# Latent attention moved to the ends of each slot, the block table cut in three, and 42 products of constants in a two-layer decoder on one core

## The chip, the core and the metric

The kernel runs on one core of a Trainium2 chip. The metric is the time of one execution in device microseconds (us). The kernel before has a median of 1145.13 us over four runs (1139.52 to 1148.7).

The engines by the profile's names: PE (TensorE matrix products; PEld is its weight load), DVE (VectorE), ACT (ScalarE), POOL (GpSimd) and SP (SyncE, which here only issues DMAs). Each engine works through its own queue in the order in which the program issued the instructions.

## What is computed

A decoder of two layers over 32 sequences of 128 tokens with 128 features. Three residual steps per layer, each with a layer norm in front:

```python
x = x + L0_attn(layernorm(x))        # 16 heads, rotary
x = x + L0_xattn(layernorm(x), ctx)  # 16 heads over 128 context tokens
x = x + L0_ffn(layernorm(x))         # gated experts, 2 of 8, and 2 shared
x = x + L1_attn(layernorm(x))        # 16 heads, rotary, causal
x = x + L1_xattn(ctx, latents=layernorm(x), mask)
x = x + L1_ffn(layernorm(x))         # relu experts, 2 of 8
```

The change touches the last two steps. `L1_xattn`, the "latent attention", has two heads of 64: queries are the normalised tokens, keys are those same tokens and 128 masked context tokens, 256 keys in all.

```python
q = ln @ Wq.T
kv = concatenate([xn @ Wkv.T, ln @ Wlkv.T])
attn = softmax(mask(rmsnorm(q) @ rmsnorm(k)))
out = attn @ v @ Wo.T + bo
```

`L1_ffn` sends each token to two of eight experts of 512 hidden features: `gate * (relu(x @ w1 + b1) @ w2 + b2)`.

## The kernel before

The 32 sequences form 8 groups (`G`) of 4 (`NG`), whose activations stay in SBUF. The three 16-head attentions run as one pipeline, written out by hand: `attention` walks over slots `k`, two slots to a sequence, 192 slots in all. A slot has the phases `open`, `pre`, then the slot's own score products and exponentials (L602 to L645), `inner`, the products with the values of an earlier pair (L661), `turn`, `turned`, `mid`, `post`. All other work is registered with `at(slot, phase, function)`, and is issued in that order; within one phase in the order of registration. The last products with values are in slot 197; after it a slot holds only what `at` put there.

The latent attention (`latent_attention`) starts for group g at slot d = 147 + 8g. After norm and projection (L1121) each of its four sequences takes four steps, at t = d + 8 + 2i for sequence i: `turn` (L1186, transposes queries and keys, which ACT copies out, L1188 and L1189) in slot t, `score` (products L1195 and L1200, maximum on DVE L1206, exponential on ACT L1207) in t + 1, `turn_e` (transposes L1214, copy on DVE L1216) in t + 2, `weigh` (products with the values L1226, division on DVE L1231 and L1232) in t + 3. `fetch` (L1181) has loaded the context's values in slot t - 2 into one of three buffers, and so waits for the `weigh` of three sequences before. `leave` (L1161) and `project` (L1168) end the group in d + 18 and d + 19. So a sequence begins every second slot from 155 to 217, with `turn` and `turn_e` in odd slots, `score` and `weigh` in even ones. All four steps are in `mid`.

The products of these steps, of norms, projections and routers share three PSUM banks (`ps_m`), taken in turn: an allocation waits until the readers of the third one before it are done; `score` takes two. The attention's own scores have two banks (`ps_s`), their transposed second form two (`ps_t`), and the sums one (`ps_a`).

After the latent attention `router` picks two experts for each token of groups (0,1), (2,3), (4,5), (6), (7), and writes the tokens by 16 or 8 indirect DMAs of POOL (`scatter`, L1729) into slots of an expert in DRAM. `expert_blocks` then works on blocks of 128 such rows, in three parts: groups 0 to 3 with 39 blocks, 4 and 5 with 23, 6 and 7 with 23. `table` (L1826 to L1852) works out on DVE, from the counts, which expert and which rows each block has. A pair of blocks takes a slot: `fetch` loads rows (L1868), `weights` copies an expert's first weights (L1877 on ACT, L1879 on DVE) out of `all_w`, `turn` transposes (L1887, copy L1889), `hidden` (L1897) and `result` (L1914) are the products, `leave` (L1928) the scatter back on POOL. `experts` gives the slots: the parts begin at `begins` = 209, 229 and 241, the table four slots earlier in `mid`; `keep` loads the eight experts' weights in slots 203 to 210 (L1966, L1967).

In `attention` (L298) `awake` issues products of an identity with itself, 128x512 in bf16, at the start of the program; nobody reads them.

Of the kernel before, what the change touches and what calls it, by code (L numbers as in the profile page):

```python
# [11 lines left out]
F32 = mybir.dt.float32  # L12
# [10 lines left out]
P = 128  # L23
# [3 lines left out]
G = B // NG  # L27
H, DH = 16, 8
E = 8
# [84 lines left out]
def decoder(ctx: ExitStack, tc: tile.TileContext, a: dict, out: bass.AP):  # L114
    nc = tc.nc
# [6 lines left out]
    ps_t = ctx.enter_context(tc.tile_pool(name="ps_t", bufs=2, space=PSUM))  # L122
# [6 lines left out]
    def bank(pool):  # L129
        return pool.tile([P, 512], F32, tag="bank", name="bank")  # L130
# [112 lines left out]
    ident_b = cpool.tile([P, P], BF16, tag="ident_b", name="ident_b")  # L243
# [3 lines left out]
    def wide(t, shape, axis):  # L247
        return t.unsqueeze(axis).to_broadcast(shape)
# [809 lines left out]
    def latent_attention(lazy, kv, row, bias, masked, plan_route):  # L1058
# [12 lines left out]
        def plan_group(at, g, d):  # L1071
# [98 lines left out]
                nc.vector.tensor_tensor(xf, ps, xf, ALU.add)  # L1170

            at(d + 18, "mid", leave)
            at(d + 19, "post", project)
            plan_route(at, g, d + 19)

        def plan_batch(at, m, g, i, t):
            b, s = g * NG + i, {}

            def fetch():
                s["kv"] = opened().tile([P, KV], F32, tag="kv", name="lkv", bufs=3)  # L1180
                nc.sync.dma_start(s["kv"][:, P:], kv[b : b + 1].rearrange("b p w -> p (b w)"))  # L1181

            def turn():
                ps = bank(ps_m)
                for n in range(2):
                    nc.tensor.transpose(ps[:, n * P : (n + 1) * P], m["qk"][:, i, n, :], ident)  # L1186
                s["qT"] = opened().tile([P, P], F32, tag="qT", name="lqT")
                nc.scalar.activation(s["qT"], ps[:, :P], AF.Identity, scale=g_qk)  # L1188
                nc.scalar.copy(s["kv"][:, :P], ps[:, P : 2 * P])  # L1189

            def score():
                sc = [bank(ps_m) for _ in range(HL)]
                rows = [slice(DL * h, DL * h + DL) for h in range(HL)]
                for h in range(HL):
                    nc.tensor.matmul(  # L1195
                        sc[h][:, P : 2 * P], ident_b[:B, b : b + 1].to_broadcast([B, P]), masked,
                        start=True, stop=False, skip_group_check=True,
                    )
                for h in range(HL):
                    nc.tensor.matmul(  # L1200
                        sc[h][:, : 2 * P], s["qT"][rows[h], :], s["kv"][rows[h], : 2 * P], start=False, stop=True, skip_group_check=True,
                    )
                mx = small.tile([P, HL], F32, tag="lmx", name="lmx")
                s["e"] = opened().tile([P, HL, 2 * P], F32, tag="e", name="le", bufs=2)
                for h in range(HL):
                    nc.vector.tensor_reduce(mx[:, h : h + 1], sc[h][:, : 2 * P], AX.X, ALU.max, negate=True)  # L1206
                    nc.scalar.activation(s["e"][:, h, :], sc[h][:, : 2 * P], AF.Exp, bias=mx[:, h : h + 1])  # L1207

            def turn_e():
                tp = bank(ps_m)  # L1210
                for h in range(HL):
                    for c in range(2):
                        n = 2 * h + c
                        nc.tensor.transpose(tp[:, n * P : (n + 1) * P], s["e"][:, h, c * P : (c + 1) * P], ident)  # L1214
                s["eT"] = opened().tile([P, 4, P], F32, tag="eT", name="leT", bufs=2)
                nc.vector.tensor_copy(s["eT"].rearrange("p n k -> p (n k)"), tp)  # L1216

            def weigh():
                if i == 0:
                    m["on"] = opened().tile([P, NG, D], F32, tag="on", name="lon", bufs=1)  # L1220
                vc = s["kv"][:, 2 * P :].rearrange("p (h w) -> p h w", h=HL)
                av = bank(ps_m)[:, : HL * (DL + 1)].rearrange("p (h w) -> p h w", h=HL)
                for h in range(HL):
                    for c in range(2):
                        v = m["v"][:, i, h, :] if c == 0 else vc[:, h, :]
                        nc.tensor.matmul(  # L1226
                            av[:, h, :], s["eT"][:, 2 * h + c, :], v,
                            start=(h == 0 and c == 0), stop=(c == 1), skip_group_check=True,
                        )
                rz = small.tile([P, HL], F32, tag="lrz", name="lrz")  # L1230
                nc.vector.reciprocal(rz, av[:, :, DL])  # L1231
                nc.vector.tensor_tensor(  # L1232
                    m["on"][:, i, :].rearrange("p (h d) -> p h d", d=DL), av[:, :, :DL], wide(rz, [P, HL, DL], 2), ALU.mult
                )

            at(t - 2, "mid", fetch)
            at(t, "mid", turn)
            at(t + 1, "mid", score)
            at(t + 2, "mid", turn_e)
            at(t + 3, "mid", weigh)  # L1240

        def beside(at, done):
            for g in range(G):
# [575 lines left out]
    def expert_blocks(f, total, lazy):  # L1819

        room, nb, top_slot = ROOM[f], NB[f], SLOTS[f] - BLOCK
        y = tc.dram_tile([2 * room, D], F32, name=f"y{f}")
        state = {}
        where = []

        def table():  # L1826

            def row(shape, tag, dtype=F32):
                return lazy["blocks"].tile([1] + shape, dtype, tag="tb_" + tag, name="tb_" + tag, bufs=2 if tag == "where" else 1)

            count, blocks, end, skip = row([E], "count"), row([E], "blocks"), row([E], "end"), row([E], "skip")
            nc.vector.tensor_tensor(count, total[:1], e_base[f][:1], ALU.subtract)
            more = row([E, room // BLOCK], "more")
            nc.vector.tensor_tensor(
                more, wide(count, [1, E, room // BLOCK], 2), wide(starts[:1, : room // BLOCK], [1, E, room // BLOCK], 1), ALU.is_gt
            )
            nc.vector.tensor_reduce(blocks, more, AX.X, ALU.add)
            upto = row([E, E], "upto")
            nc.vector.tensor_tensor(upto, wide(blocks, [1, E, E], 1), until[:1], ALU.mult)
            nc.vector.tensor_reduce(end, upto, AX.X, ALU.add)  # L1840
            nc.vector.tensor_scalar(skip, blocks, -float(BLOCK), float(room), ALU.mult, ALU.add)
            past, t = row([nb, E], "past"), row([nb, E], "past_t")
            first = row([3, nb], "first")
            nc.vector.tensor_tensor(past, wide(end, [1, nb, E], 1), wide(numbers[:1, :nb], [1, nb, E], 2), ALU.is_le)
            nc.vector.tensor_reduce(first[:, 0, :], past, AX.X, ALU.add)
            nc.vector.tensor_tensor(t, past, wide(skip, [1, nb, E], 1), ALU.mult)
            nc.vector.tensor_reduce(first[:, 1, :], t, AX.X, ALU.add)
            nc.vector.tensor_tensor(first[:, 1, :], first[:, 1, :], starts[:1, :nb], ALU.add)
            nc.vector.tensor_scalar(first[:, 2, :], first[:, 0, :], float(E - 1), 512.0, ALU.min, ALU.mult)
            nc.vector.tensor_scalar(first[:, 0, :], first[:, 0, :], float(E - 1), float(W1), ALU.min, ALU.mult)  # L1850
            where.append(row([3, nb], "where", I32))
            nc.vector.tensor_copy(where[0], first)  # L1852
# [95 lines left out]
            nc.gpsimd.tensor_tensor(one, one, two, ALU.add)  # L1948
            nc.vector.tensor_tensor(X[g], X[g], one, ALU.add)

        return table, fetch, weights, turn, hidden, result, leave, gather, finish

    def experts(halves, lazy, heads, late):

        def beside(at, done):
# [4 lines left out]
            def keep(e):  # L1960
                def fn():
                    rows = a["w_f"][e * P : (e + 1) * P]
                    if e == 0:
                        for tag, n in (("w1", W1), ("w2", 512)):
                            lazy[tag] = lazy["blocks"].tile([P, E * n], F32, tag=tag, name="all_" + tag, bufs=1)
                    nc.sync.dma_start(lazy["w1"][:, e * W1 : (e + 1) * W1], rows[:, :W1])  # L1966
                    nc.sync.dma_start(lazy["w2"][:, e * 512 : (e + 1) * 512], rows[:, W1:])  # L1967
                return fn

            at(done(2, G - 1) + 2, "open", swap)  # L1970
            for e in range(E):
                at(done(2, G - 1) + 2 + e, "open", keep(e))
            begins = [done(2, 3) + 40]
            begins.append(max(begins[0] + (NB[0] + 1) // 2, done(2, 5) + 40))
            begins.append(max(begins[1] + (NB[1] + 1) // 2, done(2, 7) + 33))

            def plan_part(f):
                table, fetch, weights, turn, hidden, result, leave, gather, finish = halves[f]
                t = begins[f]
                pairs = (NB[f] + 1) // 2  # L1980
                at(t - 4, "mid", table)
                for i in range(4):
                    at(t, "post", lambda i=i: fetch(i))
                for i in range(2):
# [95 lines left out]
    lazy, late = {}, ExitStack()  # L2080
# [123 lines left out]
```

## Time and profile before

| | us |
|---|---|
| median of four runs | 1145.13 |
| the profiled execution, its own time | 1146.88 |
| its span, first to last instruction | 1145.2 |
| last products with values (slot 197) begin | 856.4 |
| first `hidden` product (slot 211) begins | 917.3 |
| last `result` product ends | 1110.8 |

| engine | busy us | share |
|---|---|---|
| PE | 1046.9 | 91% |
| DVE | 823.7 | 72% |
| POOL | 646.1 | 56% |
| ACT | 616.1 | 54% |

The mean granted TensorE clock is 0.957. The span falls into the attention pipeline up to 857 us, a bridge of 14 slots (197 to 210) up to 917, the blocks up to 1112, and a tail with the last scatters, the gathering of the results and the stores. Rows of an engine's timeline give the start, the duration, the line, output<-input, and in square brackets how long the engine had been idle before and what ended that; "issue" is idle time without a wait.

### The profile page before, as it was taken

How to read it: one execution, taken by the hardware profiler on the slowest of the kernel's cores; microseconds unless marked ns; L12 is line 12 of the kernel's file. 1: busy time of each engine (PE TensorE's matmuls, PEld its weight loads, DVE VectorE, ACT ScalarE, POOL GpSimd, SP SyncE). 2: the span in 40 equal slices, each digit the busy share in tenths (PEclk: the TensorE clock that was granted, in tenths of full speed). 3: DMA queues.
4: the chain of work that ended last, by engine and by line, in shares of the span. 5: the costliest groups of instructions: out<-in, count | busy, mean ns of one | idle time of the engine just before them, and what ended most of it. 6: DMA issues, size and time to landing. Idle time of an engine off the chain costs nothing.

```text
span 1145.2 us, 32419 instructions
## 1 busy us (share of the span) xinstructions
PE 1046.9 (91%) x12495; PEld 817.0 (71%) x12495; DVE 823.7 (72%) x2424; ACT 616.1 (54%) x1440; POOL 646.1 (56%) x918
## 2 busy tenths in 40 slices
PE   6999999999999999999998999998997899989893
PEld 3676676777777766766676667776775588989893
DVE  4678888877787678667877768887767656766662
ACT  2355555566755565546554666674563445445551
POOL 4576666534524462444555765764884716777663
PEclk9889989999999999999999999999999679999997
DMA  7663331000120221011102000000102522223432
GB/s 205 200 192 104 104 104 63 30 29 30 38 48 5 46 48 38 10 30 39 39 3 52 2 16 16 16 12 20 39 25 81 153 53 58 65 74 98 123 98 79
DMA packets 77858, 71.24 MB, mean 62 GB/s; under 512 B 14554, under 2 KB 66829, under 8 KB 77696
## 3 DMA queue, kind: packets, MB, share of 16 engines
q1 hardware_dynamic: 72640, 60.08, 19.2%
q0 software_dynamic: 4768, 8.47, 2.2%
q8 instruction: 102, 1.67, 0.6%
q14 instruction: 60, 0.49, 0.1%
q10 hardware_dynamic: 288, 0.52, 0.1%
HBM read 33.39 MB, written 37.02 MB: 61 GB/s over the span
## 4 chain that ended last, share of the span: by engine, by line
PE 59%; DVE 17%; POOL 9%; ACT 7%; issue 4%; DMA 3%; SPq 1%; DVEq 0%; POOLq 0%; ACTq 0%
PE bank L633 13%; PE bank L661 6%; PE bank L1914 6%; PE bank L1897 5%; DVE msc L636 4%; PE bank L950 3%; POOL h L941 2%; PE bank L932 2%; DMA g<-spread 2%; ACT e L644 2%; PE bank L933 2%; PE bank L486 2%; PE bank L511 1%; PE bank L1121 1%; PE bank L298 1%
## 5 line engine op out<-in xcount | busy, mean ns | idle before, releaser
L644 ACT ACTIVATE e<-bank 128x512 f32<-128x512 f32 x384 | 207.4, 593 | 173.3 <-PE bank L633 171.7
L636 DVE TENSOR_REDUCE msc<-bank 128x4 f32<-128x512 f32 x384 | 245.0, 679 | 71.2 <-PE bank L633 68.6
L633 PE MATMUL bank<-kb,qz 32*128 32x256 f32 x1536 | 243.6, 410 | 11.7 <-DVE msc L636 9.9
L633 PE MATMUL bank<-qa,kb 32*128 32x128 f32 x3072 | 235.1, 290 | 4.0 <-ACT e L644 3.9
L633 PEld LDWEIGHTS bank<-qa,kb 32*128 32x128 f32 x3072 | 196.2, 192 | 8.1 <-ACT e L644 7.2
L633 PEld LDWEIGHTS bank<-kb,qz 32*128 32x128 f32 x1536 | 147.7, 190 | 64.1 <-DVE msc L636 32.6
L1928 POOL DMA_INDIRECT y<-bo,bx x85 | 85.2, 1002 | 63.2 <-ACT bo L1921 40.9
L647 POOL TENSOR_SCALAR_AFFINE_SELECT e<-e 128x512 f32<-128x512 f32 x128 | 79.5, 646 | 67.5 <-ACT e L644 67.2
L661 PE MATMUL bank<-e,vt 128*32 128x128 f32 x3072 | 109.6, 285 | 0.9 <-POOL e L647 0.8
L661 PEld LDWEIGHTS bank<-e,vt 128*32 128x32 f32 x3072 | 81.6, 113 | 15.9 <-POOL e L647 2.0
L1914 PE MATMUL bank<-all_w,bh 128*128 x680 | 87.8, 284 | 0.5 <-issue 0.4
L1914 PEld LDWEIGHTS bank<-all_w,bh 128*128 128x128 f32 x680 | 83.0, 199 | 2.7 <-issue 2.3
L1897 PE MATMUL bank<-bxT,w 128*128 128x128 f32 x680 | 84.9, 278 | 0.0
L1729 POOL DMA_INDIRECT slots<-rows,r_ati x64 | 63.8, 997 | 33.1 <-issue 17.4
L1897 PEld LDWEIGHTS bank<-bxT,w 128*128 128x128 f32 x680 | 81.2, 196 | 0.0
L941 POOL TENSOR_TENSOR h<-h,g 128x512 f32<-128x512 f32 x30 | 38.7, 1301 | 67.1 <-DMA g<-spread 40.4
L338 ACT ACTIVATE xn<-x,ln_nb,ln_rs 128x128 f32<-128x128 f32 x96 | 42.0, 490 | 47.4 <-POOL ln_nb L332 46.9
L1207 ACT ACTIVATE le<-bank,lmx 128x256 f32<-128x256 f32 x64 | 26.8, 470 | 60.7 <-DVE lmx L1206 60.7
L1905 DVE TENSOR_SCALAR bh<-bank,w 128x128 f32<-128x128 f32 x164 | 46.1, 343 | 17.5 <-PE bank L1897 17.0
L540 DVE SCALAR_TENSOR_TENSOR qa<-bank,head_rows,qz 128x128 f32<-128x128 f32 x192 | 57.6, 342 | 0.0
L1903 ACT ACTIVATE bh<-bank,w 128x128 f32<-128x128 f32 x176 | 50.3, 368 | 10.6 <-PE bank L1897 8.7
L1921 ACT ACTIVATE bo<-bank,bx 128x128 f32<-128x128 f32 x44 | 16.2, 367 | 65.4 <-PE bank L1914 65.4
(337 smaller groups left out, 2309.8 us busy)
## 6 DMA issues: line engine op xcount, KB each, us to landing
slots<-nowhere SPq DMA_DIRECT2D x8, 1170.0 KB, 10.9
slots<-nowhere SPq DMA_DIRECT2D x4, 2210.0 KB, 20.6
g<-spread SPq DMA_DIRECT2D x16, 512.0 KB, 5.2
bx<-slots SPq DMA_DIRECT2D x85, 65.0 KB, 1.9
kv<-kcv SPq DMA_DIRECT2D x8, 516.0 KB, 3.2
lkv<-kv SPq DMA_DIRECT2D x32, 129.0 KB, 2.1
yg<-y SPq DMA_DIRECT2D x14, 256.0 KB, 4.4
all_w<-in_w_f SPq DMA_DIRECT2D x8, 258.0 KB, 3.3
```

The costliest lines, as they stand in the source:

```text
L540: nc.vector.scalar_tensor_tensor(s["qa"][:, u, :], s["mp"], head_rows[:, 1 - u : 2 - u], m["qz"][:, u, i * P : (i + 1) * P], ALU.mult, ALU.add
L633: nc.tensor.matmul(o, l, r, start=start, stop=stop, skip_group_check=True)
L636: nc.vector.tensor_reduce(tops(MSC[bb % 4], 2 * h + j), sc[j].rearrange("p (s n k) -> p s n k", s=2, n=2), AX.X, ALU.max, negate=True)
L644: nc.scalar.activation(e.rearrange("p n q -> p (n q)"), tr[j], AF.Exp, scale=SCALE)
L647: nc.gpsimd.affine_select(out=e, in_=e, compare_op=ALU.is_ge, fill=0.0, base=0, pattern=[[0, 4], [1, P]], channel_multiplier=-1)
L661: nc.tensor.matmul(s3["av"][32 * n : 32 * n + 32, h3 * P : (h3 + 1) * P], m3["vt"][:, i3, h3, n, u, :], es[u][:, n, :], start=(h3 == 0 and ...
L941: engine.tensor_tensor(m["h"][:, c, :], m["h"][:, c, :], m["g"][:, c, :], ALU.mult)
L1729: ins = nc.gpsimd.indirect_dma_start(slots[f], bass.IndirectOffsetOnAxis(ap=m["ati"][:, c, n : n + 1], axis=0), m["rows"][c][:, n, :], Non ...
L1897: nc.tensor.matmul(ps[:, c * P : (c + 1) * P], w[:, c * P : (c + 1) * P], s["xT"][:, u * P : (u + 1) * P], start=True, stop=True)
L1903: nc.scalar.activation(h, p, AF.Relu, bias=bias)
L1914: nc.tensor.matmul(ps[:, u * P : (u + 1) * P], s["h"][:, u, c, :], lazy["w2"][:, bass.ds(at_w + c * P, P)], start=(c == 0), stop=(c == 3),)
L1928: ins = nc.gpsimd.indirect_dma_start(y, bass.IndirectOffsetOnAxis(ap=x[:, D : D + 1].bitcast(U32), axis=0), s["o"][:, u, :], None, bounds_ ...
```

## The change

Four edits: `project` goes from `post` to `mid` (`g >= 0` holds for every group); the latent steps `turn` and `score` go from `mid` to `pre` and `turn_e` and `weigh` from `mid` to `post`, in the same slots; `table` becomes three functions in `post` of three slots in a row; and three products of constants are put in each of the slots 197 to 210, 42 in all.

```diff
             at(d + 18, "mid", leave)
-            at(d + 19, "post", project)
+            at(d + 19, "mid" if g >= 0 else "post", project)
...
             at(t - 2, "mid", fetch)
-            at(t, "mid", turn)
-            at(t + 1, "mid", score)
-            at(t + 2, "mid", turn_e)
-            at(t + 3, "mid", weigh)
+            early, late = ("pre", "post") if g >= 0 else ("mid", "mid")
+            at(t, early, turn)
+            at(t + 1, early, score)
+            at(t + 2, late, turn_e)
+            at(t + 3, late, weigh)
...
-        def table():
+        def table_counts():
             count, blocks, end, skip = row([E], "count"), row([E], "blocks"), row([E], "end"), row([E], "skip")
...
             nc.vector.tensor_reduce(blocks, more, AX.X, ALU.add)
-            upto = row([E, E], "upto")
+
+        def table_ends():
+            blocks, end, skip, upto = tb["blocks"], tb["end"], tb["skip"], row([E, E], "upto")
...
             nc.vector.tensor_reduce(first[:, 0, :], past, AX.X, ALU.add)
+
+        def table_firsts():
+            past, first, skip, t = tb["past"], tb["first"], tb["skip"], row([nb, E], "past_t")
             nc.vector.tensor_tensor(t, past, wide(skip, [1, nb, E], 1), ALU.mult)
...
+            def awake():
+                nc.tensor.matmul(
+                    bank(ps_t).rearrange("p (n k) -> p n k", n=4), ident_b, wide(ident_b, [P, 4, P], 1), start=True, stop=True
+                )
+
+            for k in range(done(2, G - 1) - 4, begins[0] + 2):
+                for phase in ("open", "inner", "post"):
+                    at(k, phase, awake)
...
-                at(t - 4, "mid", table)
+                for n, table in enumerate(tables):
+                    at(t - 4 + n, "post", table)
```

Instruction by instruction, the queues of POOL and SP hold the same operations in the same order as before. PE's has 42 weight loads and 42 products more; PE, DVE and ACT issue the latent attention's operations, and DVE the table's, at other places.

More of the change, by code (lines that the diff above doesn't have):

```diff
@@ L1824, in expert_blocks, with row @@
         where = []
-        def table():
-            def row(shape, tag, dtype=F32):
-                return lazy["blocks"].tile([1] + shape, dtype, tag="tb_" + tag, name="tb_" + tag, bufs=2 if tag == "where" else 1)
+        tb = {}
+        def row(shape, tag, dtype=F32):
+            tb[tag] = lazy["blocks"].tile([1] + shape, dtype, tag="tb_" + tag, name="tb_" + tag, bufs=2 if tag == "where" else 1)
+            return tb[tag]
+        def table_counts():
             count, blocks, end, skip = row([E], "count"), row([E], "blocks"), row([E], "end"), row([E], "skip")
@@ L1841, in table @@
             nc.vector.tensor_scalar(skip, blocks, -float(BLOCK), float(room), ALU.mult, ALU.add)
-            past, t = row([nb, E], "past"), row([nb, E], "past_t")
-            first = row([3, nb], "first")
+            past, first = row([nb, E], "past"), row([3, nb], "first")
             nc.vector.tensor_tensor(past, wide(end, [1, nb, E], 1), wide(numbers[:1, :nb], [1, nb, E], 2), ALU.is_le)
             nc.vector.tensor_reduce(first[:, 0, :], past, AX.X, ALU.add)
+        def table_firsts():
+            past, first, skip, t = tb["past"], tb["first"], tb["skip"], row([nb, E], "past_t")
             nc.vector.tensor_tensor(t, past, wide(skip, [1, nb, E], 1), ALU.mult)
@@ L1949, in finish @@
             nc.vector.tensor_tensor(X[g], X[g], one, ALU.add)
-        return table, fetch, weights, turn, hidden, result, leave, gather, finish
+        return (table_counts, table_ends, table_firsts), fetch, weights, turn, hidden, result, leave, gather, finish
     def experts(halves, lazy, heads, late):
@@ L1968, in keep @@
                 return fn
+            begins = [done(2, 3) + 40]
+            begins.append(max(begins[0] + (NB[0] + 1) // 2, done(2, 5) + 40))
+            begins.append(max(begins[1] + (NB[1] + 1) // 2, done(2, 7) + 33))
+            def awake():
[5 more added lines that the diff above has]
+                    at(k, phase, awake)
             at(done(2, G - 1) + 2, "open", swap)
@@ L1972, in beside @@
                 at(done(2, G - 1) + 2 + e, "open", keep(e))
-            begins = [done(2, 3) + 40]
-            begins.append(max(begins[0] + (NB[0] + 1) // 2, done(2, 5) + 40))
-            begins.append(max(begins[1] + (NB[1] + 1) // 2, done(2, 7) + 33))
             def plan_part(f):
-                table, fetch, weights, turn, hidden, result, leave, gather, finish = halves[f]
+                tables, fetch, weights, turn, hidden, result, leave, gather, finish = halves[f]
                 t = begins[f]
                 pairs = (NB[f] + 1) // 2
-                at(t - 4, "mid", table)
+                for n, table in enumerate(tables):
+                    at(t - 4 + n, "post", table)
                 for i in range(4):
```

## The prediction

> **What bounds the kernel now.** I read the stages first (busy time in stretches), then the PE timeline for its waits, then the chain of waits, then POOL's timeline where the chain leaves PE. Columns of the first view: stretch, its length, PE, PEld, DVE, ACT, POOL busy (instructions), granted clock, DMA share, GB/s.
>
> ```profile
> 640.00:857.00 217.00, 200.66 (x2789) 155.26 (x2784) 169.88 (x482) 130.25 (x318) 147.22 (x222) 0.97 0.07 19
> 857.00:917.00 60.00, 46.95 (x269) 32.70 (x259) 41.86 (x138) 25.90 (x69) 34.66 (x44) 0.78 0.39 116
> 917.00:1112.00 195.00, 184.02 (x1550) 177.53 (x1551) 126.28 (x444) 98.60 (x278) 118.96 (x131) 0.96 0.30 82
> ...
> 884.00:900.00 16.00, 13.61 (x56) 10.04 (x57) 10.06 (x37) 6.04 (x16) 12.46 (x19) 0.50 0.77 227
> ```
>
> PE is the bound outside the bridge: 16 us idle of 217 before it, 11 of 195 after it. In the bridge PE is idle 13 of 60, and 16 us ran at half clock. So the reorder can win parts of 16 us, and the bridge is where more could lie.
>
> The waits of PE in one turn of eight slots, and the worst beside a router:
>
> ```profile
> 688.41 0.44 PE L1186 MATMUL bank<-ident,lqk 128*128 128x128 f32 x2 [0.54 <-ACT qz L456]
> 700.36 0.21 PE L1195 MATMUL bank<-masked,ident_b 32*128 32x128 bf16 x1 [0.51 <-ACT vt L491]
> 702.22 1.16 PE L1168 MATMUL bank<-w_xo,loT 128*128 128x128 f32 x8 [0.43 <-ACT le L1207]
> 712.53 1.66 PE L1121 MATMUL bank<-w_lat,lT 128*128 128x384 f32 x4 [0.71 <-DVE lon L1232]
> ...
> 784.08 0.63 PE L1111 MATMUL bank<-ident,lat 128*128 128x128 f32 x4 [2.98 <-DVE lon L1232]
> ```
>
> Each waits for a `ps_m` bank that a neighbour in the same `mid` still holds: 2.2 us per turn.
>
> The end of the bridge in the chain of waits, and POOL before it:
>
> ```profile
> 907.82 0.26 POOL r_nb L1621
> ...
> 913.17 2.85 DMA all_w<-in_w_f
> 916.04 0.43 DVE w L1879
> 916.47 0.34 DVE bxT L1889
> 916.86 0.69 PE bank L1887 x2
> 917.55 3.41 PE bank L1897 x16
> ```
>
> ```profile
> 878.01 1.68 POOL L1139 TENSOR_TENSOR nrml<-nrml,half 128x8 f32<-128x8 f32 x1 [5.22 <-DVE nrml L997]
> 879.88 1.04 POOL L1729 DMA_INDIRECT slots<-rows,r_ati  x1 [0.20 <-issue]
> ...
> 904.39 0.97 POOL L1729 DMA_INDIRECT slots<-rows,r_ati  x1 [0.30 <-issue]
> ...
> 907.82 0.26 POOL L1621 TENSOR_SCALAR r_nb<-r_nb 128x8 f32<-128x8 f32 x1
> ```
>
> From 878.0 to 908.1 POOL waits for nobody: 14 scatters at 1.28 us from start to start (17.9), two roots of 1.68, nine norm steps (4.4), a bias add (1.3), four router steps (2.6) are 29.6 of 30.1 us. Then SP issues the block fetches, 0.83 each, until 913.1, then the last weights (2.85), then copies, then L1897. From 878 on the bridge hangs on POOL and SP, whose queues the change leaves in order; PE's half clock from 884 to 900 lies beside POOL.
>
> **The change part by part.**
>
> *Latent steps to `pre` and `post`, slots 155 to 197* (some 5.2 turns of 38.8 us). Nothing is added; places change. I followed the three banks round a turn in the new order. Gone: the waits for `vt`, `le` and `lon`, because `score` takes its banks three microseconds before `values` or `project` wants one, and `weigh` a slot's end before L1121: 1.65 a turn. The `qz` wait changes place: `score` in slot 4 of the turn needs the banks of queries and keys, read by ACT for 1.49 and 0.63: 0.5. New: `score` in slot 0 needs the bank whose copy (L506, 0.58) stands on ACT behind the squares (L994, 0.63) and those behind L1122 (0.42): 1.85 after the last L1121 product against 1.0 of PE work, 0.85. New: in `pre` the latent maximum (0.75) stands on DVE ahead of the attention's own maxima (1.28), and the latent exponentials (0.84) on ACT ahead of the attention's own, for which PE's next slot waits: 0.3 by the lag of 1 to 1.5 us that I find in slot 2, nothing elsewhere. Net -2.2 + 1.65 = -0.55 a turn, -2.5 in four plain turns. By a router, the norm's transposes (L1111) now come ahead of `weigh`, so the 2.98 goes, and of the 1.8 after it I leave all: -2 net with the same new waits. Sum -4.5. Ends: -9 (no new wait) and +3 (new waits double, router gains nothing).
>
> For the first half the page's row speaks:
>
> ```profile
> L1207 ACT ACTIVATE le<-bank,lmx 128x256 f32<-128x256 f32 x64 | 26.8, 470 | 60.7 <-DVE lmx L1206 60.7
> ```
>
> ACT stands 60.7 us in front of 64 latent exponentials, as the maximum lies on DVE behind the slot's maxima and `qa`. In `pre` it lies behind the last slot's rest only.
>
> *The bridge.* POOL's run starts with the root that needs L997 (877.25). Between the router's places (to 869.98) and L997 lie 7.3 us of DVE, of which 0.69, 0.95 and 0.66 are waits for `weigh`, `score` and L1121; with `weigh` behind L997 and `score` a phase earlier I take 2.4 off. The run and what follows move by the same: -2.4. Ends: -5.2 (all of POOL's wait), and +2.6: 12 awake products of slots 197 to 200 on the path at 0.216 (twelve in 2.76 at the start).
> The other 30 products (6.5 us) I cost at nothing: PE's work in slots 201 to 207 at full-clock rows (four times 0.44 and 0.22 for `turn_e` and `turn`, three times 0.9 and 0.89 for `weigh` and `score`, 2.2 and 0.5 for the router, 0.44, 0.44, 0.9 and 1.6 for L1161, L1111, L1168, L1121) is 14 us, 18.6 with 21 constants, beside the 27.4 that POOL takes up to the last scatter. If that cover were gone they cost up to 6.5. `fetch` (L1181) now waits for a `weigh` at the slot's end, behind it on SP the weight loads and block fetches; the last went at 903.86, 2.95 ahead of the first block fetch (906.81). Two L1121 (1.9) and a product come in between, 2.1, so nothing; uncovered 2.1.
>
> *Clock.* From 884 to 900 the clock is 0.50 though PE's longest idle in the 24 us before is 1.59 us: it is the share of work, not one long gap, that let it fall. Constants raise that share. What they save on the path is the first block: 3.41 against 1.79, 1.6. In slot 214 `project` waits 1.71 for `lon` (941.63), then runs cold: 1.96 against 0.9, and the next L1914 2.59 against 1.8; `project` in `mid` comes ahead of that: up to 3.6. But PE still waits some 4 us for weights at the end of the bridge, behind the last constant. Of 5.2 I take half: -2.5; ends 0 and -5.2.
> [...]
>
> *The table.* Part 0: 3.85 us of DVE (892.96 to 896.81) beside POOL's run: 0. Part 1 (1003.89 to 1007.1): PE's next wait (1.85) is for rows that need POOL's r_nb, not the table: 0. Part 2 (1059.18 to 1063.64): PE waits 1.54 for `bxT` behind it (1065.22): -1.5, as pieces of 0.65, 1.4 and 1.55 us fit into DVE's free 1.5 us of a 3.8 us slot. Ends 0 and -3. The table is ready two slots later, still 7 us ahead of SP's use.
>
> Sum: -4.5 - 2.4 - 2.5 - 1.5 = -10.9. The profiled execution took 1146.88 (span 1145.2 and 1.7 around it): 1136.0. It lies 1.75 above the median, so 1134 against 1145.13. The terms' ends give -22 to +6; unlikely to meet, I take 1127 to 1141 as this case's own range.
>
> **The rivals.** *Slower: latent exponentials in the way.* At 723.69 ACT had waited 2.57 for the latent maximum. If in `pre` that wait stays, the attention's exponentials of 21 even slots start that much later; between such a pair's end (721.1) and the next slot's second products (722.1) is 1.0 us. 1.57 x 21 = 33 in all slots, 16 in half: with -6.4 of the other parts +10 to +27, 1155 to 1172. It decides from 0.85 us per even slot. For it: DVE is busy 78% there, its maxima ran 3 us late at 726. Against: the latent maximum passes most of that queue.
> *Much faster: PE sets the bridge.* Then clock and idle count in full: PE's busy time at full clock is some 36 of 60 (46.95 x 0.78), with constants 45, so -15 there, -8.5 elsewhere: 1121. Against it POOL's unbroken run.
> *No gain: the constants do on the path what they cost.* If DVE's steps to 873 and PE alternate, all 42 x 0.216 = 9.1 come in, in place of -2.4: 1145.7. Against it: they have no input to wait for and run while PE waits.
>
> **How the numbers follow.** Under 1% (11.5 us) cannot be told from no change here. First case 0.58, half of it beyond 1133.7; much faster 0.16; no gain 0.11; slower 0.15. Faster: 0.29 + 0.16 = 0.45; same: 0.29 + 0.11 = 0.40; slower 0.15. The range 1120 to 1150 leaves out most of the slower case and some of the fastest: 0.2.
>
> **What would show it.** PE's waits on `vt`, `le` and `lon` before L1195, L1168 and L1121 gone, new ones before L1195 on ACT `oT` and `k`, idle of L1207 well under 60; POOL's run from root to r_nb still about 30 us, beginning about 2.4 us earlier after slot 197's products; a higher clock in the bridge without a bridge shorter by more than 5 us; no PE wait on `bxT` behind the third table. It is wrong if the stretch up to slot 197 changes by over 9 us, or if POOL's run breaks.

## The result, and the profile after

| | before | after |
|---|---|---|
| median, us (runs) | 1145.92 (78) | 1149.64 (52) |
| lowest to highest | 1138.66 to 1151.49 | 1143.3 to 1159.51 |
| ratio, 95% interval | 1 | 1.0039 [1.0027, 1.0051] |
| the profiled execution, its span | 1146.88, 1145.2 | 1147.23, 1145.4 |

The changed kernel is 4.5 us slower (0.0039 x 1145.92; by the interval 3.1 to 5.8) where 11 us less were forecast. The profiled execution of after lies 2.4 us under its median, that of before 1.0 above its own, so the loss isn't seen in the two spans and has to be looked for by stages. (The last `result` product of before ends at 1125.6, not at 1110.8; in after it ends at 1125.5.) The first view is the busy time in stretches, columns as before:

```profile
640.00:857.00 217.00, 200.51 (x2798) 153.90 (x2796) 171.14 (x490) 132.12 (x321) 148.01 (x224) 0.98 0.07 19
857.00:917.00 60.00, 48.23 (x272) 31.77 (x271) 39.87 (x127) 22.99 (x60) 33.15 (x41) 0.88 0.35 104
917.00:1112.00 195.00, 183.29 (x1549) 176.92 (x1550) 125.57 (x447) 98.74 (x279) 118.58 (x131) 0.96 0.31 85
884.00:900.00 16.00, 13.02 (x69) 8.49 (x68) 7.84 (x22) 5.42 (x14) 12.78 (x19) 0.85 0.65 192
```

Between 640 and 857 PE is idle 16.5 us of 217, as before (16.3): no wait has been saved on balance. In the bridge the granted clock went from 0.78 to 0.88, and from 0.50 to 0.85 between 884 and 900. PE's timeline shows which waits took the place of the old ones:

```profile
685.45 0.21 PE L1195 MATMUL bank<-masked,ident_b 32*128 32x128 bf16 x1 [0.24 <-ACT qz L456]
685.92 0.21 PE L1195 MATMUL bank<-masked,ident_b 32*128 32x128 bf16 x1 [0.26 <-ACT k L464]
...
705.24 0.21 PE L1195 MATMUL bank<-masked,ident_b 32*128 32x128 bf16 x1 [0.62 <-DVE leT L1216]
...
710.54 0.44 PE L1226 MATMUL bank<-lv,leT 128*128 128x65 f32 x2 [0.55 <-ACT lv L1123]
...
788.27 0.66 PE L1214 MATMUL bank<-ident,le 128*128 128x128 f32 x4 [2.50 <-ACT lv L1123]
```

The first two are the forecast wait of `score` for the queries and keys, 0.50 together as forecast. The third stands where 0.85 was forecast behind the copy of `oT`, but the copy of `leT` ends it. The fourth was not forecast, and neither was the last: by a router, the 2.98 in front of L1111 is gone and 2.50 stands in front of L1214 instead. ACT's exponentials wait less, as forecast, while PE's idle total stays:

```profile
L1207 ACT ACTIVATE le<-bank,lmx 128x256 f32<-128x256 f32 x64 | 26.7, 467 | 40.3 <-DVE lmx L1206 40.3
```

In the bridge POOL's run begins 2.1 us earlier after slot 197's products with values (854.57 here, 856.37 before), and then it breaks:

```profile
874.10 1.68 POOL L1139 TENSOR_TENSOR nrml<-nrml,half 128x8 f32<-128x8 f32 x1 [5.69 <-DVE nrml L997]
...
901.30 0.97 POOL L1730 DMA_INDIRECT slots<-rows,r_ati  x1 [0.30 <-issue]
905.22 0.25 POOL L1619 TENSOR_SCALAR r_rs<-r_mv 128x8 f32<-128x8 f32 x1 [2.94 <-DVE r_mv L1614]
...
907.58 0.26 POOL L1622 TENSOR_SCALAR r_nb<-r_nb 128x8 f32<-128x8 f32 x1
```

From the start of the last scatter to that of r_nb it was 3.4 us, now 6.3. POOL waits for the router's statistics (r_mv), and these stand on DVE. Before, DVE had them ready in time:

```profile
903.25 0.28 DVE L1612 BATCH_NORM_STATS2 ln_st<-x 128x6 f32<-128x128 f32 x1
...
903.97 0.18 DVE L1613 BATCH_NORM_AGGREGATE r_mv<-ln_st 128x2 f32<-128x6 f32 x1
```

The last of them ended at 904.15, and POOL came to them at 905.44: 1.3 us to spare. After the change DVE first waits for the late `weigh`:

```profile
897.29 0.17 DVE L1231 RECIPROCAL lrz<-bank 128x2 f32<-128x2 f32 x1 [4.85 <-PE bank L1226]
```

The chain of waits shows what stands behind that. Before, its last links to SP were POOL's, from r_rs at 905.44 to r_nb; now they are DVE's.

```profile
895.76 1.50 PE bank L1226 x8
897.49 0.29 DVE lon L1232
898.14 1.59 DVE tb_skip L1847
899.74 0.40 DVE tb_past L1849
900.16 0.47 DVE tb_first L1850
901.43 0.64 DVE lqk L1122 x2
902.07 0.60 DVE leT L1216
902.67 0.39 DVE tb_past_t L1854
903.08 0.48 DVE tb_first L1855
905.12 0.32 DVE lmx L1206
...
908.07 0.30 DVE lon L1232
908.37 0.30 SPq L1863
...
...
915.32 2.63 DMA all_w<-in_w_f
...
919.48 3.42 PE bank L1905 x16
```

The second and third piece of part 0's table are links of it, 3.3 us of the tb_ rows shown; then a `lon` at 908.07, which is the `weigh` of slot 208 at the slot's end, and behind it SP's reads of the table (L1863) and block fetches. Both were costed at nothing. The products of the first block still take 3.42 (3.41 before).

### The profile page after: what moved, and what is told of

The parts are those of the page before. It is cut to its first block, busy times and chain, and to the rows that moved or that the text cites. A ratio compares the mean times of both kernels' runs of the same rounds, so it can differ in the third digit from the quotient of the medians.

```text
span 1145.4 us, 32485 instructions
## 1 busy us (share of the span) xinstructions
PE 1046.4 (91%) x12537; PEld 811.3 (71%) x12537; DVE 821.9 (72%) x2424; ACT 615.9 (54%) x1440; POOL 645.0 (56%) x918
## 3 DMA queue, kind: packets, MB, share of 16 engines
q8 instruction: 102, 1.67, 0.6%
## 4 chain that ended last, share of the span: by engine, by line
PE 52%; DVE 16%; POOL 13%; ACT 8%; issue 6%; DMA 4%; SPq 1%; POOLq 0%; DVEq 0%; ACTq 0%
PE bank L633 12%; PE bank L1922 6%; PE bank L1905 5%; PE bank L661 5%; DVE msc L636 4%; PE bank L950 3%; DMA g<-spread 3%; POOL h L941 2%; POOL slots L1730 2%; ACT e L644 2%; PE bank L932 2%; PE bank L1226 2%; POOL e L647 1%; PE bank L933 1%; PE bank L298 1%
## 5 line engine op out<-in xcount | busy, mean ns | idle before, releaser
L633 PEld LDWEIGHTS bank<-kb,qz 32*128 32x128 f32 x1536 | 145.0, 188 | 64.7 <-DVE msc L636 33.7
L647 POOL TENSOR_SCALAR_AFFINE_SELECT e<-e 128x512 f32<-128x512 f32 x128 | 79.8, 648 | 74.8 <-ACT e L644 74.7
L661 PEld LDWEIGHTS bank<-e,vt 128*32 128x32 f32 x3072 | 80.4, 112 | 14.8 <-POOL e L647 1.6
L1730 POOL DMA_INDIRECT slots<-rows,r_ati x64 | 64.0, 999 | 31.1 <-issue 16.5
```

The costliest lines, as they stand in the source:

```text
L633: nc.tensor.matmul(o, l, r, start=start, stop=stop, skip_group_check=True)
L647: nc.gpsimd.affine_select(out=e, in_=e, compare_op=ALU.is_ge, fill=0.0, base=0, pattern=[[0, 4], [1, P]], channel_multiplier=-1)
L661: nc.tensor.matmul(s3["av"][32 * n : 32 * n + 32, h3 * P : (h3 + 1) * P], m3["vt"][:, i3, h3, n, u, :], es[u][:, n, :], start=(h3 == 0 and ...
L1730: ins = nc.gpsimd.indirect_dma_start(slots[f], bass.IndirectOffsetOnAxis(ap=m["ati"][:, c, n : n + 1], axis=0), m["rows"][c][:, n, :], Non ...
```

## The experiments

All were timed against the kernel before on the same chip. The five chips differ: on two, the kernel before takes 1146 to 1147 us, on three 1179 to 1181, so ratios are compared, and stages of the blocks only between chips of one kind. The theory at the start: the late `weigh` stands on PE behind the norm's transposes (L1111), DVE waits with it, and the statistics come late to POOL. Its rival: the constants cost on the path what they take. That the pieces of parts 0 and 1 stand on DVE in front of the router's statistics and picks became the theory only after the third run.

**Parts of the change, one at a time.** Latents alone, with `project` in `mid`:

```diff
-            at(t, "mid", turn)
-            at(t + 1, "mid", score)
-            at(t + 2, "mid", turn_e)
-            at(t + 3, "mid", weigh)
+            at(t, "pre", turn)
+            at(t + 1, "pre", score)
+            at(t + 2, "post", turn_e)
+            at(t + 3, "post", weigh)
```

> The kernel before with the latent steps (and project) moved alone; table whole in mid, no constants. Theory A (the attention gains about 4 us, and the bridge gives it back because weigh, now at the end of slot 206, stands on PE behind the norm's transposes L1111, which wait for POOL; DVE waits with it, and the router's statistics and POOL's r_nb come late): slot 191 about 4 us earlier than before, r_nb no earlier than in the kernel before, first block within 2 us of before's 919.4; with the whole table still ahead of that wait, r_nb should come 1 to 3 us earlier than in the changed kernel. Time 1143 to 1149. Theory B (the 42 constants cost their 9 us on the path): clearly faster, 1138 to 1141, as the constants are not there.

Measured 0.9991 [0.9968, 1.0014]. The latents don't explain the loss, and their gain can't be told from none.

Constants alone:

```diff
+            for k in range(done(2, G - 1) - 4, begins[0] + 2):
+                for phase in ("open", "inner", "post"):
+                    at(k, phase, awake)
```

> The kernel before with the 42 products of constants alone. Theory A (POOL and SP set the bridge, PE has room): r_nb and the first block within 1 us of before, granted clock of the bridge higher, time within 2 us of before. Theory B (constants on the path): the bridge 4 to 9 us longer, time 1150 to 1155. Theory C (the clock matters): bridge 2 to 5 us shorter, time 1140 to 1143.

Measured 0.9999 [0.9979, 1.0019], with the granted clock in the bridge at 0.92.

The table alone:

```diff
-                at(t - 4, "mid", table)
+                for n, table in enumerate(tables):
+                    at(t - 4 + n, "post", table)
```

> The kernel before with the table in three pieces alone. Theory A: part 2's wait of PE for bxT (1.5 us) goes, nothing in the bridge (weigh is ahead of L1111 here, so DVE does not wait): -1 to -2 us. If the pieces themselves are what holds DVE in the bridge: r_nb 1 to 3 us later than before and time +1 to +3 us.

Measured 1.0060 [1.0037, 1.0083], 1154.51 us, 6.9 us slower, and slower than the whole change; last scatter to r_nb 6.83. Neither expectation reached that: the edit that was to gain 1.5 us is the one that loses.

The changed kernel with `weigh` of the last two groups back in `mid`:

```diff
-            at(t + 3, late, weigh)
+            at(t + 3, late if g < 6 else "mid", weigh)
```

> The changed kernel with weigh of groups 6 and 7 back in mid, all else as changed; on PE this only puts weigh ahead of L1111 in slot 206 and ahead of L1121 in slot 208 (and the like in group 7). Theory A: DVE's wait of 4.85 us for weigh goes, POOL's 2.94 us for the router's statistics goes, r_nb near 905 (changed kernel 907.6), first block 2.5 to 3.5 us earlier than in the changed kernel, time 3 to 5 us under it. Theory B (constants): no different from the changed kernel, 1149 to 1150.

Measured 1.0007 [0.9981, 1.0032]: some 3.7 us of the loss came back by the medians' ratio (0.0032 x 1146), although the intervals overlap a little. So the late `weigh` has a share too.

**Undoing the pieces of parts 0 and 1, and their place.** In the changed kernel, whole tables in slots 205 and 225, pieces for part 2 alone:

```diff
-                    at(t - 4 + n, "post", table)
+                    at(t - 4 + (n if f == 2 else 0), "post" if f == 2 else "mid", table)
```

> The changed kernel with the tables of parts 0 and 1 whole again, at the place of the kernel before (slots 205 and 225, `mid`); part 2's stays in pieces. Theory A (the pieces of parts 0 and 1 stand on DVE ahead of the router's statistics and picks): the gap between POOL's last scatter and r_nb falls from 6.3 to under 4.7 us, the 47.7 us with part 1's table return to within 0.7 of the kernel before, and the time is 5 to 7 us under the changed kernel's 1149.6: 1143 to 1145, ratio 0.997 to 0.999. Theory B (weigh behind the norm's transposes breaks POOL's run, the pieces only follow it): only part 1's 2.6 us come back, the gap stays over 5.5: 1146.5 to 1148, ratio 1.001 to 1.002.

Measured 0.9978 [0.9952, 1.0005]; POOL from last scatter to r_nb 3.41. Against the changed kernel's 1.0039 that is 0.6% (7 us of 1146), the theory's size. But this run was on a chip of the second kind and the changed kernel only on chips of the first, so the comparison of the two ratios is a guide and no proof; the 3.41 us is.

The same with groups 6 and 7 wholly as before (`g < 6` in place of `g >= 0`, for the latents and for `project`):

> As the run before it, and the latents of groups 6 and 7 also back in `mid`, their project in `post`; groups 0 to 5 early and late, 42 constants kept. Theory A: the attention's 2.7 to 3.9 us and part 2's 1.6 stay, the bridge is that of the kernel before: 1140 to 1142, ratio 0.995 to 0.997. Theory B: the same here, as the weigh of groups 6 and 7 is in its old place; the two part only in what this run gains on the one before it: 2 to 3 us by A, 3 to 5 by B. If the attention's gain in the traces is only noise of single executions: 1144 to 1145.

Measured 0.9959 [0.9937, 0.9982]. Its POOL and SP at the end of the bridge, on the same axis of time:

```profile
901.12 0.97 POOL L1730 DMA_INDIRECT slots<-rows,r_ati  x1 [0.30 <-issue]
902.17 0.25 POOL L1619 TENSOR_SCALAR r_rs<-r_mv 128x8 f32<-128x8 f32 x1
```

```profile
902.21 0.33 SPq L1181 DMA_DIRECT2D lkv<-kv  x1
904.00 6.25 SPq L1876 DMA_DIRECT2D bx<-slots  x8
```

POOL goes on at once, and the block fetch comes 2.9 us after the last scatter (2.4 before, 7.7 after the change).

The same without the 42 constants:

> As the run before it without the 42 constants. If constants neither cost nor save (ratio 0.9999 when they were added alone): within 1.5 us of the run before it, with the granted clock in the bridge back from near 0.88 to near 0.78. If the clock of the bridge is on the path: 2 to 5 us longer. If the constants stand in PE's way: 2 to 5 us shorter.

Measured 0.9993 [0.9968, 1.0018], above the 0.9959 of the run beside it, with intervals that overlap; repeated below.

The kernel before, whole table two slots later, where the last piece stood:

```diff
-                at(t - 4, "mid", table)
+                at(*((t - 4, "mid") if f == 2 else (t - 2, "post")), table)
```

> The kernel before with the tables of parts 0 and 1 whole but two slots and a phase later, at the end of slots 207 and 227, where the last piece stood; part 2's where it was. Place (what stands on DVE ahead of the statistics and picks there delays POOL and the fetches behind it): 4 to 9 us slower, ratio 1.003 to 1.008, r_nb over 5 us after the last scatter. Cutting (three pieces at three places each meet a wait, a whole one meets one): within 1.5 us of the kernel before.

Measured 1.0088 [1.0059, 1.0117], over the upper end of what was expected; last scatter to r_nb 6.21. It is the place that costs; the cutting isn't needed for it.

**Controls and repeats.** The kernel before against itself:

> The kernel before, unchanged, against itself: it shows how far the ratio and the stages of one profiled execution scatter on this chip. Every theory: ratio 0.998 to 1.002; stages without chance in them (last scatter to r_nb 3.4 us, part 2's table 24.4) within 0.3 us of the first profile, the attention with its waits within 4.

Measured 1.0021 [0.9996, 1.0046], just over the expected range: one ratio of this kind can be off by 0.2%.

The versions for groups 0 to 5, with and without constants, once more:

> The version with early and late latents for groups 0 to 5, constants, and pieces for part 2 alone, once more. If its gain is real: ratio 0.994 to 0.998, slots 155 to 191 shorter by 1.5 to 4 us than in the run of the kernel before on this chip, part 2's stage by 1.6. If its first ratio of 0.9959 was luck: 0.998 to 1.001.

> The same without the 42 constants, once more; the first pair differed by 3.6 us, with intervals that overlap. Constants neither cost nor save: ratio within 0.001 of the run before it. Constants shorten the way from slot 191 to the first block (by 1.4 us in the first pair): 0.001 to 0.003 above it, and the stage again 1 to 2 us longer.

Measured 0.9987 [0.9960, 1.0014] and 0.9983 [0.9955, 1.0011]. The two are equal this time: the first pair's 0.0034 did not come again, and 0.9987 lies where it was expected if the first run's 0.9959 was luck.

The version for groups 0 to 5 with part 1's table in pieces:

> As the version for groups 0 to 5, with constants, and part 1's table in three pieces as in the changed kernel, part 0's whole. If the pieces stand in the way of the router's picks of unit 7: the stage with part 1's table (blocks 14 to 24) 2 to 4 us longer than without them on this chip, and the ratio 0.002 to 0.003 higher. If part 1's 2.6 us in the changed kernel came from elsewhere: within 0.7 us.

Measured 0.9985 [0.9959, 1.0011], no dearer than without. A miss: on this kind of chip PE lost so much time in that stretch for another reason (last section) that 2.6 us more or less don't show: the stretch took 58.2 us here and 59.0 in the run beside it without the pieces.

**One part's pieces at a time**, on a chip of the first kind, in the kernel before (`n if f == 0 else 0`, and `"post" if f == 0 else "mid"`, likewise 1 and 2):

> The kernel before with part 0's table alone in three pieces. Theory A (pieces ahead of the statistics break POOL's run): last scatter to r_nb over 5 us in place of 3.4, 3 to 6 us slower, ratio 1.003 to 1.005. Rival (the break is made up before the end, by the first blocks waiting for weights anyway): gap over 5, ratio within 0.0015 of 1.

Measured 1.0046 [1.0017, 1.0076]. DVE, then POOL, then SP in that run:

```profile
905.06 1.99 DVE L1845 TENSOR_TENSOR tb_upto<-tb_blocks,until 1x64 f32<-1x64 f32 x1
...
908.22 0.27 DVE L1613 BATCH_NORM_STATS2 ln_st<-x 128x6 f32<-128x128 f32 x1
...
910.25 0.46 DVE L1854 TENSOR_TENSOR tb_past_t<-tb_past,tb_skip 1x312 f32<-1x312 f32 x1
...
911.77 0.21 DVE L1860 CAST tb_where<-tb_first 1x117 int32<-1x117 f32 x1
911.91 0.27 DVE L1613 BATCH_NORM_STATS2 ln_st<-x 128x6 f32<-128x128 f32 x1
```

```profile
905.67 1.29 POOL L1106 TENSOR_TENSOR x<-x,bias_l 128x512 f32<-128x512 f32 x1
...
908.42 0.97 POOL L1730 DMA_INDIRECT slots<-rows,r_ati  x1 [0.30 <-issue]
912.89 0.25 POOL L1619 TENSOR_SCALAR r_rs<-r_mv 128x8 f32<-128x8 f32 x1 [3.49 <-DVE lrz L1231]
```

```profile
910.90 0.33 SPq L1181 DMA_DIRECT2D lkv<-kv  x1
912.77 6.25 SPq L1876 DMA_DIRECT2D bx<-slots  x8
```

With everything else as before, the second piece stands ahead of the first statistics (L1613) and the third ahead of the second ones; POOL waits 3.49 us for the latter, and SP issues the first fetch 0.8 us after the table's last instruction. "7 us ahead of SP's use" had become nothing.

> The kernel before with part 1's table alone in three pieces. Theory A (pieces ahead of unit 7's picks and statistics): 2 to 4 us slower, ratio 1.002 to 1.004, all of it in blocks 14 to 24, the bridge as before. Rival (the stretch absorbs it): within 0.0015 of 1.

Measured 1.0040 [1.0017, 1.0063]; from block pair 14's first relu to pair 24's 50.35 us (47.71 before). All of it is in one pair (7.75 in place of 5.25). PE with part 1's pieces, and then, from the run with part 2's pieces alone, the same place without them:

```profile
1027.12 1.95 PE L1905 MATMUL bank<-bxT,w 128*128 128x128 f32 x16
1030.72 0.18 PE L1702 MATMUL bank<-r_both,above_b 128*128 128x32 bf16 x1 [1.65 <-DVE r_both L1687]
...
1031.30 3.33 PE L1922 MATMUL bank<-all_w,bh 128*128 x16 [0.31 <-issue]
1034.42 1.45 PE L1905 MATMUL bank<-bxT,w 128*128 128x128 f32 x8
```

```profile
1024.82 1.95 PE L1905 MATMUL bank<-bxT,w 128*128 128x128 f32 x16
1027.52 0.18 PE L1702 MATMUL bank<-r_both,above_b 128*128 128x32 bf16 x1 [0.75 <-DVE r_both L1687]
...
1028.04 2.11 PE L1922 MATMUL bank<-all_w,bh 128*128 x16 [0.25 <-issue]
1029.99 1.06 PE L1905 MATMUL bank<-bxT,w 128*128 128x128 f32 x8
```

The pieces delay the picks of unit (7) (r_both) by 0.9 us; after the longer gap the granted clock is 0.72 from 1030 to 1036 us (1.00 from 1027 to 1033 in the other run), and the 16 products and the next 8 take 1.2 and 0.4 us more. 0.9 + 1.2 + 0.4 = 2.5.

> The kernel before with part 2's table alone in three pieces. As predicted: 1.5 us faster, ratio 0.998 to 0.9995, blocks 24 to 30 shorter by 1.6 where PE waited for bxT behind the table, all else as before. If nothing: 1.000.

Measured 0.9995 [0.9971, 1.0019]; pairs 24 to 30 took 22.81 in place of 24.43, as expected, but 1.6 us is under what the ratio can tell.

> The changed kernel itself. Its ratio was 1.0039: 1.002 to 1.006 here, last scatter to r_nb 5 to 6.5 us, slots 155 to 191 shorter by 3 to 4.5 us than in the kernel before.

Measured 1.0039 [1.0021, 1.0057], the first result again; last scatter to r_nb 6.83, somewhat over the expected 5 to 6.5.

**The two costs taken out of the change.**

> Early and late latents for groups 0 to 5, constants, pieces for part 2 alone, a third time. If it is a real gain: 0.995 to 0.998. If not: 0.999 to 1.001.

Measured 0.9998 [0.9971, 1.0025]. The three runs of this version, 0.9959, 0.9987 and 0.9998, average 0.9981, and two of the three meet the expectation of no gain: a gain over the kernel before isn't secured. All three were on chips of the second kind, the changed kernel (1.0039 twice) on the first, so that this version beats the changed kernel is likely and not shown.

> The changed kernel with the tables of parts 0 and 1 whole in their old place and the weigh of groups 6 and 7 in `mid`; scores and turns of all groups stay early, constants stay. If late weigh and pieces are the whole of the loss, POOL's run begins early and stays unbroken: last scatter to r_nb under 4.7 us, last scatter to the block fetch under 3.5, slot 191 to the first block 1 to 3 us shorter than in the version for groups 0 to 5, ratio 0.993 to 0.997. If the early scores of groups 6 and 7 give back what they gain: as that version or worse, 0.997 to 1.000.

Measured 0.9997 [0.9968, 1.0026]. POOL's run is whole (3.41) and the fetch comes 2.8 us after the last scatter, but slot 191 to the first block is longer than in the run beside it (93.4 against 88.7 us). The ratio fits the second expectation, that the early scores of groups 6 and 7 give back what they gain, which asks for other marks than those of the expectations.

## Why the prediction was wrong, point by point

The terms that failed were those put at nothing, the table's pieces of parts 0 and 1 and the late fetch (together +7.6 measured), and two gains that didn't come, -4.5 of the latent steps and -2.5 of the clock.

The expectations judge the attention's gain by the time from DVE's maximum of slot 155 to that of slot 191. That mark was badly chosen, since it stops six slots before the last products with values. Below, marks are the starts of the first product with values of score slots 152 (issued in slot 159), 180 (slot 187) and 191 (the last, slot 197), then POOL's root before the last 14 scatters, the last scatter, and the first relu of block pairs 0, 14, 24 and 30. Means over all profiled executions that have, or have not, the edit concerned (the difference in the first row is known to some 1 us, by the scatter of the executions):

| stretch, us | without | with | predicted | measured |
|---|---|---|---|---|
| products 152 to 191 (latents; 8 and 12 executions) | 194.3 | 194.4 | -4.5 | +0.1 |
| of it, 152 to 180 | 149.8 | 146.0 | | -3.8 |
| of it, 180 to 191 | 44.5 | 48.4 | | +3.9 |
| products 191 to root (same) | 21.7 | 19.3 | -2.4 | -2.4 |
| root to last scatter (same) | 26.6 | 27.2 | 0 | +0.6 |
| last scatter to pair 0 (12 without late `weigh` and part 0's pieces; the changed kernel twice) | 15.5 | 20.5 | 0, clock -1.6 | +5.0 |
| pairs 14 to 24 (first kind of chip; 5 and 5) | 47.9 | 50.5 | 0 | +2.6 |
| pairs 24 to 30 (same) | 24.4 | 22.8 | -1.5 | -1.6 |

The measured column, without the two rows that split the first, adds to +4.3; the ratio gives +4.5. So near an agreement is partly luck, as the first row alone is uncertain by 1 us, but nothing of size is left over. Single spans could not have shown it: the time up to the first mark, nearly all of which the change leaves alone, runs from 658 to 670 us in the twenty profiles.

- *Latent steps.* The step "-0.55 a turn" had the right sign: one plain turn takes 38.76 without and 38.50 with the change, to 0.04 in all but one execution, so -0.26. (And four times 0.55 is 2.2, not the 2.5 of the sum.) "-2 net" by a router held where it was read: the six slots 181 to 186, beside the router of (0,1), went from 40.0 to 38.0 in the mean, the 2.50 in front of L1214 included. What failed is that the slots after it were costed as no worse than plain ones. Slots 187 to 192 went from 29.0 to 30.4 and slots 193 to 196, beside the router of (2,3), from 14.8 to 17.1: +3.8, and all that had been won is given back. PE idles 4.3 us in these ten slots in place of 1.8, in many small waits; in after's first profile none is over 0.74. About half of the rest is work that now comes ahead of the last mark, two constants and a `turn` (0.65). I have no run that takes one of the new waits away alone, so which of the moved steps causes them stays open. The condition of the slower rival, exponentials in the way, wasn't met.
- *POOL's run earlier.* -2.4 held. "If POOL's run breaks" was named as what would make the prediction wrong, and it broke.
- *`fetch` behind the late `weigh`.* "So nothing; uncovered 2.1" failed: with late `weigh` and the table whole, last scatter to pair 0 took 18.3 and 17.4 (latents alone; whole tables), 2.3 over the 15.5. It was the delay that was mis-sized, not the cover of 2.95: the latent fetch went from 0.5 us ahead of the last scatter (903.86 and 904.39) to 6.5 behind it (907.81 and 901.30), 7 us, where two L1121 and a product had been counted, 2.1; `weigh` in `post` also lies behind L1111, the norm on POOL and the table's pieces. Without pieces ahead of it the fetch went 4.4 and 3.4 us behind the last scatter (latents alone; whole tables), still more than the cover.
- *Table, part 0.* "3.85 us of DVE beside POOL's run: 0" failed, and so did "still 7 us ahead of SP's use": 20.2 in both runs with the pieces and `weigh` in `mid` as before, +4.7. The whole table stood two slots ahead of the statistics, and after it DVE still waited 2.55 us for the products of L1168 (900.42, L1170). At the new places DVE's next work is what POOL and SP wait for, with 1.3 us to spare for some 3 us of table. The "7 us" could have been read off too: the third piece's place is at the second statistics (903.25 in the rows of before), so its 1.7 us would end some 2 us ahead of the first block fetch (906.81), as an estimate from these rows. The two costs overlap: together +5.0, not 7. With early scores and `weigh` in `mid` the same pieces cost 2.0 (17.5), so the price seems to hang on how close DVE is to POOL's next need; that is one run.
- *Table, part 1.* "0" failed, +2.6, of which 0.9 is the wait and the rest the clock behind it in the run shown. In two of the five executions (the changed kernel's first among them) the clock behind this wait stayed full and the other 1.2 us fell in pair 15 instead, where it was granted 0.54 in place of 0.68. I had looked only at the next wait of PE after the whole table, not at the router's picks beside the new places.
- *Table, part 2.* -1.5 held, -1.6.
- *Constants and clock.* "Of 5.2 I take half" failed: nothing. The clock of the bridge rose to 0.86 to 0.92 in ten profiles of kernels with constants, against 0.72 to 0.79 in ten without, and the time stayed (0.9999 alone; 0.9987 and 0.9983 with and without, on one chip). That the share of work let the clock fall was the author's estimate; the runs show only that it was higher with the constants. Last scatter to pair 0 was 15.3 with and 15.2 without, in the version for groups 0 to 5. The argument in the forecast against its own fastest rival, that PE waits for POOL, SP and weights anyway, held also for the 1.6 of the first block: in both profiles of the changed kernel PE still idles 2.2 and 4.1 us in front of it and takes 3.62 for its 16 products, as before. Nor did `project` in `mid` show: pairs 0 to 14 took 79.3 to 79.8 with it, 79.4 to 82.6 without, on the first kind of chip.

The rival "no gain" (1145.7) came nearest in time and had another cause: the constants on the path. They cost nothing there. No rival had the mechanism that decided.

## What to carry to other kernels

A step that costs nothing where it stands isn't free elsewhere: before moving it, list what is next in the same engine's queue at the new place, and who waits for that. Here some 3 us of tiny instructions in front of a router's statistics, which had 1.3 us to spare, cost 4.7, as POOL's run and SP's fetches hung on them. A delay behind a moved step is the wait for everything issued ahead of it at the new place, on every engine that it passes (7 us here, not 2.1). And a gain between two marks is only a gain if the second lies behind all the work that was shifted.

## What the runs showed of the hardware

**Tiny DVE instructions that took long beside a POOL add.** tb_upto, 64 elements, took 0.21 us in the kernel before and 1.99 in the run with part 0's pieces, from 905.06 to 907.05; POOL's 128x512 add (L1106, above) ran from 905.67 to 906.96. In the changed kernel tb_skip (0.15 before) took 1.67 and ended at 899.74, the add at 899.71. In the kernel before, tb_count of part 2 took 1.18 (0.15 in part 0) and ended at 1060.36, a POOL add of 128x512 (L1948) at 1060.33. Each time the DVE instruction ends within 0.1 us of the POOL add. The rows of tb_upto and tb_skip begin 0.6 and 0.35 us before that of the add, that of tb_count 0.15 after it. What ties the two engines together there isn't shown.

**Behind a gap of some 1.65 us the clock was lower once, and once not.** In the run with part 1's pieces the 16 products behind a wait of 1.65 took 3.33, at a granted clock of 0.72 from 1030 to 1036; in the changed kernel's first profile much the same wait, 1.62, left them at 2.22 and the clock at 1.00. No run here shows what decides it.

**Slow issue on PE on some chips.** On the chips where the kernel before takes 1179 to 1181 us, 30 of the 36 us between its two profiles (spans 1180.9 and 1145.2) lie in pairs 0 to 24: PE is idle 18 us more there and busy 12 us more, at a granted clock of 0.87 against 0.99 from 960 to 1080 us. In most of that idle time PE waited for nothing that the profile shows and issued a product every 0.7 us, as here in the version for groups 0 to 5:

```profile
1003.98 0.27 PE L1922 MATMUL bank<-all_w,bh 128*128 x1 [0.24 <-issue]
1004.70 0.36 PE L1922 MATMUL bank<-all_w,bh 128*128 x1 [0.45 <-issue]
```

The kernel before shows it on such a chip too, in the group of L1897 (instructions, busy time, mean ns, idle before): 10.3 us of idle, where its first profile has 0.0.

```profile
L1897 PE MATMUL bank<-bxT,w 128*128 128x128 f32 x680 | 92.5, 290 | 10.3 <-issue 7.9
```

What holds the issue up there isn't known.
